# Layer 0 beside layer 1: which engine adds the blocks of exponentials into the softmax sums

## Chip, cores and metric

The kernel runs on one core of a Trainium2 chip. The metric is device time in microseconds (us), the median of three runs; before the change it is 3661.74 us (3661.73 to 3662.2). The profiled execution spans 3658.6 us. PE is TensorE, DVE is VectorE, ACT is ScalarE, POOL is GpSimd and SP is the queue that issues the DMAs.

## The reference

The input is a float32 image batch of 4 x 256 channels x 48 x 48. Four layers follow one another, each as `x = x + layer(group_norm(x))`:

- Layer 0 is attention over the 2304 pixels with 8 heads of 64 channels. Queries and keys are normalised to length one.
- Layer 1 is a pooled, blurred, depthwise attention gate.
- Layer 2 is attention with one head of 64 channels, then a batch norm over the whole batch.
- Layer 3 is a channel gate, a depthwise 3x3 convolution and an instance norm.

What matters here is layer 0:

```python
sim = jnp.einsum('bhdi,bhdj->bhij', q, k) * SCALE
attn = jax.nn.softmax(sim, axis=-1)
out = jnp.einsum('bhij,bhdj->bhid', attn, v)
out = out.transpose(0, 1, 3, 2).reshape(b, HEADS * DIM_HEAD, h, w)
return jnp.einsum('oc,bchw->bohw', w_out, out) + b_out[None, :, None, None]
```

The softmax needs, for every query, the sum of its 2304 exponentials. That sum is what the change is about.

## The kernel before

**Units.** Layer 0 is cut into units. A unit is one image (`b`, 0 to 3), one pair of heads (`p`, 0 to 3) and one chunk of 384 queries (`c`, 0 to 5), so there are 96 units, 24 for each image. A unit goes over 18 blocks of 128 keys, in 9 groups (`g`) of two blocks. For each block PE multiplies keys and queries (`scores`, L270), ACT takes the exponential of the 128 x 768 result into a tile `pt` (L276; there are eight such tiles), and PE multiplies it with the values (`weigh`, L290).

**Sums.** The same `pt` tiles are added up into one 128 x 768 tile `acc` for each unit, by `add_up` (L295 to L316). For groups in the unit's `paired` set, GpSimd first adds the group's two blocks into a tile `half` (L301), and VectorE adds `half` to `acc` one group later. For other groups, VectorE adds both blocks itself. The first add of a unit has no `acc` yet and adds two blocks (L310). With `PAIRED = (1, 3, 5, 7)` the adds fall like this:

| | GpSimd | VectorE |
|---|---|---|
| group 0 | | L310, one add of two blocks |
| groups 1, 3, 5, 7 | one pair add each (L301) | nothing |
| groups 2, 4, 6, 8 | | L316 three times: the waiting `half`, then two blocks |

That is 4 adds on GpSimd and 13 on VectorE for each unit.

**Order.** The order of the instructions on every engine is written by hand: the function `attend` (L427) walks over all groups of all units, and engines work their own list in that order. One step of it is called a slot here; a unit has slots 0 to 8. In a slot come, in this order: the scores of this group, `add_up` of the group before, what is `due`, then what fills TensorE (`fills`) and the steps of layer 1 that run beside it (`lanes`), and last the `weigh` of the group before:

```python
            for j in range(g * G, (g + 1) * G):
                scores(u, j)
            do(fills, t, lambda rank: rank < 1)
            if prev is not None:
                add_up(*prev)
            do(due, t)
```

So the adds of group g are in slot g + 1, and those of group 8 in slot 0 of the next unit.

**After a unit.** `last` (L407) sets the rest of a unit by slots counted from slot 0 of the next unit: in slot 2 GpSimd adds two halves of the output (`fold`, L367); in slot 3 TensorE sums `acc` over the partitions (`total`, L323); in slot 5 VectorE inverts the sums (`invert`, L343 to L358) and DMAs spread them over the partitions; in slot 0 of the unit after (9 slots on) GpSimd multiplies with them (`divide`, L371); and in slot 2 of that unit (11 slots on) comes `out_proj`. It has two parts, each a product on TensorE (L648, two matmuls) and an add on VectorE from PSUM into the image `X` (L653). The PSUM tiles `pj` come from a pool of two, shared with the projections of the next pair of heads. In slot 2 their order on TensorE is: a query projection (L566), the values (L597), `out_proj` part 0, a key projection (L566), `out_proj` part 1. So part 1 takes the `pj` tile of part 0, and its matmul waits until L653 of part 0 has read it.

**Layer 1 beside layer 0.** While the units of image b run, for b = 1, 2, 3, layer 1 of image b - 1 runs in the same slots. Its steps on VectorE are, for each of two channel halves: maxima and blur (L765 to L797, two steps in slot 2 and one each in slots 3, 5, 6 and 8, some 18 us in all), rounds of tap products (written by ACT, L826, summed by VectorE with one reduce of 1.48 us, L849, in slots 2, 4, 6 and 8), and the gate (L936 to L956). Image 0 has nothing of layer 1 beside it.

Of the kernel before, what the change touches and what calls it, by code (L numbers as in the profile page):

```python
# [22 lines left out]
SL = 384  # L23
# [42 lines left out]
PAIRED = (1, 3, 5, 7)  # L66
# [8 lines left out]
def usual_path(  # L75
# [566 lines left out]
    def out_proj(b, p, c, pair, o):  # L642

        cols = slice(c * SL, (c + 1) * SL)

        def part(k):
            ps = pj_tile()
            nc.tensor.matmul(  # L648
                ps[:, :SL], lhsT=wo[:, p, k * P : (k + 1) * P], rhs=o["o"], start=True,
                stop=True,  # L650
            )
            xs = X[b][:, k, cols]
            nc.vector.scalar_tensor_tensor(  # L653
                xs, ps[:, :SL], pair["bo"][:, k : k + 1], xs, ALU.add, ALU.add
            )

        return [((2.5 if b else 0, 4)[k], lambda k=k: part(k)) for k in range(NK)]

    def l0_unit(b, p, c, pair):
        hold = {}  # L660

        def o_tile():
            hold["o"] = op.tile([P, SL], F32, tag="o", name="o")
            return hold["o"]

        return {
            "pt": {}, "qc": slice(c * SL, (c + 1) * SL), "paired": PAIRED,
            "soon": b == B - 1 and p == NPAIR - 1 and c == NCH - 1,
            "scale": 1.0, "of": pair, "o": o_tile,
            "after": out_proj(b, p, c, pair, hold),  # L670
        }
# [555 lines left out]
    for i, (b, p) in enumerate(order):  # L1227
# [30 lines left out]
        if p == 1 and b + 1 < B:  # L1258
            others.append((gn(b + 1, norms0[b + 1], placed=True), NSL + 1, 0, n - 3 * NG))
        phases.append(([l0_unit(b, p, c, pairs[b][p]) for c in range(NCH)], work, others))  # L1260

    n = L2C * NG
# [1261 lines left out]
```

## Time and profile before

| | PE | DVE | ACT | POOL |
|---|---|---|---|---|
| busy us of the 3658.6 us span | 3499.3 | 2617.0 | 2381.9 | 1389.8 |
| share | 96% | 72% | 65% | 38% |

The main rows for the adds, over the whole span (layer 2 uses the same lines):

| line | engine, operation | count | mean |
|---|---|---|---|
| L301 | POOL, half = pt + pt | 477 | 1990 ns |
| L316 | DVE, acc = acc + pt | 792 | 1215 ns |
| L316 | DVE, acc = acc + half | 459 | 1035 ns |
| L310 | DVE, acc = pt + pt | 99 | 1521 ns |

A group's row in the profile gives the busy time, the mean of one instruction, and the idle time of its engine just before it with what ended most of that. A window view gives busy times for stretches of the span. The timeline gives single instructions with their start and length; a bracket holds the idle time before, and who ended it. Layer 0 beside layer 1 is the stretch from 759 us to 2945 us (72 units); from 78 us to 759 us layer 0 runs alone.

### The profile page before, as it was taken

How to read it: one execution, taken by the hardware profiler on the slowest of the kernel's cores; microseconds unless marked ns; L12 is line 12 of the kernel's file. 1: busy time of each engine (PE TensorE's matmuls, PEld its weight loads, DVE VectorE, ACT ScalarE, POOL GpSimd, SP SyncE). 2: the span in 40 equal slices, each digit the busy share in tenths (PEclk: the TensorE clock that was granted, in tenths of full speed). 3: DMA queues.
4: the chain of work that ended last, by engine and by line, in shares of the span. 5: the costliest groups of instructions: out<-in, count | busy, mean ns of one | idle time of the engine just before them, and what ended most of it. 6: DMA issues, size and time to landing. Idle time of an engine off the chain costs nothing. (4 is left out here: it accounts for less than half of the span.)

```text
span 3658.6 us, 86475 instructions
## 1 busy us (share of the span) xinstructions
PE 3499.3 (96%) x36338; PEld 1778.0 (49%) x36338; DVE 2617.0 (72%) x3227; ACT 2381.9 (65%) x3814; POOL 1389.8 (38%) x881
## 2 busy tenths in 40 slices
PE   8999999999999999999999999999999999999685
PEld 4555555454444445544444444444444445654343
DVE  3555555476989786869896868688967687576687
ACT  4665666666875886668758866687588555555353
POOL 2333333333333333333333333333333366664232
PEclk9999999999999999999999999999999999999797
DMA  2111111111111111311111111111111100000001
GB/s 91 47 25 21 27 22 25 21 25 21 26 21 25 21 26 21 77 21 25 21 25 21 25 21 26 21 26 21 30 13 30 13 6 6 6 8 4 26 39 66
DMA packets 113534, 95.52 MB, mean 26 GB/s; under 512 B 56192, under 2 KB 110064, under 8 KB 111600
## 3 DMA queue, kind: packets, MB, share of 16 engines
q1 hardware_dynamic: 110240, 87.73, 13.1%
q8 instruction: 286, 4.69, 0.5%
q10 hardware_dynamic: 2896, 2.18, 0.2%
q14 instruction: 112, 0.92, 0.1%
HBM read 56.97 MB, written 11.80 MB: 19 GB/s over the span
## 5 line engine op out<-in xcount | busy, mean ns | idle before, releaser
L276 ACT ACTIVATE pt<-sc 128x768 f32<-128x768 f32 x1944 | 1475.3, 811 | 768.2 <-PE sc L270 759.9
L301 POOL TENSOR_TENSOR half<-pt 128x768 f32<-128x768 f32 x477 | 948.7, 1990 | 1607.9 <-ACT pt L276 1512.2
L270 PE MATMUL sc<-q,k 64*64 64x384 f32 x13824 | 1273.3, 483 | 5.1 <-ACT pt L276 5.1
L290 PE MATMUL av<-pt,v 64*64 64x384 f32 x13824 | 1276.4, 484 | 0.0
L316 DVE TENSOR_TENSOR acc<-acc,pt 128x768 f32<-128x768 f32 x792 | 962.1, 1215 | 81.0 <-DVE acc L316 1.9
L270 PEld LDWEIGHTS sc<-q,k 64*64 64x64 f32 x13824 | 521.0, 133 | 607.9 <-issue 537.3
L290 PEld LDWEIGHTS av<-pt,v 64*64 64x64 f32 x13824 | 518.6, 133 | 592.2 <-issue 559.5
L316 DVE TENSOR_TENSOR acc<-acc,half 128x768 f32<-128x768 f32 x459 | 475.1, 1035 | 306.3 <-POOL half L301 305.1
L653 DVE SCALAR_TENSOR_TENSOR x<-pj,bo,x 128x384 f32<-128x384 f32 x192 | 118.3, 616 | 435.3 <-PE pj L648 434.8
L826 ACT ACTIVATE prod<-pd,wt 128x256 f32<-128x256 f32 x486 | 335.9, 761 | 0.2
L566 PE MATMUL pj<-xs,w 128*128 128x384 f32 (+1 forms) x720 | 275.4, 505 | 0.9 <-POOL xs L510 0.9
L371 POOL TENSOR_TENSOR o<-o,rinv 128x384 f32<-128x384 f32 x95 | 119.0, 1253 | 358.0 <-DMA rinv<-rinv 336.1
L566 PEld LDWEIGHTS pj<-xs,w 128*128 128x128 f32 x720 | 124.1, 189 | 128.9 <-issue 35.9
L290 PE MATMUL av<-pt,qv 64*64 64x384 f32 x1728 | 178.0, 503 | 0.0
L648 PE MATMUL pj<-o,wo 128*128 128x384 f32 x384 | 162.0, 506 | 14.8 <-DVE x L653 7.2
L270 PE MATMUL sc<-qv,kd 64*64 64x384 f32 x1728 | 172.3, 491 | 2.4 <-ACT pt L276 2.4
L849 DVE TENSOR_REDUCE prod<-prod 128x256 f32<-128x1280 f32 x114 | 168.4, 1477 | 4.1 <-ACT prod L826 4.1
L310 DVE TENSOR_TENSOR acc<-pt 128x768 f32<-128x768 f32 x99 | 150.6, 1521 | 10.7 <-ACT pt L276 10.7
L597 PEld LDWEIGHTS pj<-w,xs 128*128 128x128 f32 x1080 | 134.5, 191 | 24.1
L597 PE MATMUL pj<-w,xs 128*128 128x128 f32 x1080 | 134.9, 275 | 0.0
L367 POOL TENSOR_TENSOR o<-raw 128x384 f32<-128x384 f32 x95 | 117.6, 1238 | 0.0
L582 ACT ACTIVATE k<-pj,bias 128x384 f32<-128x384 f32 x90 | 52.3, 581 | 95.3 <-PE pj L566 94.8
(234 smaller groups left out, 2672.0 us busy)
## 6 DMA issues: line engine op xcount, KB each, us to landing
xs<-in_x_dram SPq DMA_DIRECT2D x90, 384.0 KB
rinv<-rinv SPq DMA_DIRECT2D x208, 94.5 KB
out_dram<-x SPq DMA_DIRECT2D x6, 1152.0 KB
l<-row SPq DMA_DIRECT2D x416, 1.5 KB
w<-in_wqkv_dram SPq DMA_DIRECT2D x32, 192.0 KB
x<-in_x_dram SPq DMA_DIRECT2D x4, 1152.0 KB
x<-in_x_dram SPq DMA_DIRECT2D x9, 384.0 KB
rinv<-ls SPq DMA_DIRECT2D x208, 1.5 KB
```

The lines of the kernel that those rows point to most:

```text
L270: nc.tensor.matmul(ps[c * D : (c + 1) * D, h, :SL], lhsT=u["of"]["k"][r, j0 : j0 + D], rhs=u["of"]["q"][r, u["qc"]], start=True, stop=True,)
L276: nc.scalar.activation(pt, ps[:, :, :SL], AF.Exp, scale=u["scale"])
L290: nc.tensor.matmul(u["av"][h * D : (h + 1) * D, half, :SL], lhsT=value(u, j, h)[r], rhs=pt[r, h, :], start=j == 0, stop=j == JB - 1,)
L301: nc.gpsimd.tensor_add(half, pts[0], pts[1])
L310: nc.vector.tensor_add(u["acc"], ready[0], ready[1])
L316: nc.vector.tensor_add(u["acc"], u["acc"], term)
L371: eng.tensor_mul(o, o, u["rinv"])
L566: nc.tensor.matmul(ps[:, :n], lhsT=at["w"][:, k, t, :], rhs=xs[s][:, k, :n], start=k == 0, stop=k == NK - 1,)
L597: nc.tensor.matmul(ps[:, i * P : (i + 1) * P], lhsT=xs[s][:, k, i * P : (i + 1) * P], rhs=at["w"][:, k, 2, :], start=k == 0, stop=k == NK - 1,
L648: nc.tensor.matmul(ps[:, :SL], lhsT=wo[:, p, k * P : (k + 1) * P], rhs=o["o"], start=True, stop=True,)
L826: nc.scalar.activation(bufs[n % 3][:, :, min(n, 1) + i].rearrange("p (r c) -> p r c", c=AS), pd[:, PAD + dr : PAD + dr + AS, PAD + dc : PA ...
L849: nc.vector.tensor_reduce(to, bufs[n % 3][:, :, : min(n, 1) + len(taps)], AX.X, ALU.add)
```

## The change

For the units of images 1 to 3, those that run beside layer 1, the set of paired groups is empty: VectorE adds both blocks of every group itself, and GpSimd adds no pairs there. Units of image 0 keep their pairs, and so does layer 2, which has its own setting. The aim is to take GpSimd's pair adds away from beside VectorE's work of layer 1.

```diff
         return {
-            "pt": {}, "qc": slice(c * SL, (c + 1) * SL), "paired": PAIRED,
+            "pt": {}, "qc": slice(c * SL, (c + 1) * SL), "paired": () if b else PAIRED,
             "soon": b == B - 1 and p == NPAIR - 1 and c == NCH - 1,
             "scale": 1.0, "of": pair, "o": o_tile,
```

## The prediction

> **What bounds the kernel now.** I read the page's first part, then windows by image, the waits of TensorE, the groups of VectorE by form, and a timeline. The windows below are layer 0 of image 0 alone, then images 1, 2 and 3 beside layer 1; columns are the window and its length, then the busy time and instructions of each engine.
>
> ```profile
> PE 3499.3 (96%) x36338; PEld 1778.0 (49%) x36338; DVE 2617.0 (72%) x3227; ACT 2381.9 (65%) x3814; POOL 1389.8 (38%) x881
> ...
> 77.50:759.20 681.70, 681.02 (x7400) 343.43 (x7392) 357.04 (x490) 415.07 (x659) 230.19 (x165) 1.00 0.16 28
> 759.20:1487.80 728.60, 722.20 (x7730) 355.17 (x7722) 577.62 (x672) 528.72 (x856) 267.69 (x157) 1.00 0.15 24
> 1487.80:2216.60 728.80, 721.45 (x7732) 355.47 (x7724) 572.54 (x675) 528.71 (x856) 265.15 (x158) 1.00 0.16 29
> 2216.60:2945.00 728.40, 716.69 (x7728) 351.01 (x7724) 563.66 (x653) 524.36 (x834) 261.85 (x156) 1.00 0.14 21
> ```
>
> TensorE sets the time. It idles 0.7 us in image 0 and 6.4, 7.4 and 11.7 us in images 1 to 3: 25.5 us is all the idle time that any edit there can return. VectorE is busy 79% beside layer 1, so it matters only where TensorE waits for it. TensorE's waits in the stretch 760 to 2945 us (total, times, longest):
>
> ```profile
> PE pj L648 <- DVE x L653: 6.9, 6, 1.7
> ...
> PE pj L196 <- DVE x L653: 2.8, 3, 1.0
> ...
> PE pj L1029 <- DVE bias L983: 2.5, 1, 2.5
> ...
> PE pj L566 <- POOL xs L510: 0.9, 1, 0.9
> ```
>
> VectorE's lateness costs 6.9 + 2.8 + 2.5 = 12.2 us, in ten places. Nowhere does ScalarE wait for a `pt` tile. Why VectorE is late, by its groups and GpSimd's in the same stretch:
>
> ```profile
> L316 DVE TENSOR_TENSOR acc<-acc,pt 128x768 f32<-128x768 f32 x576 | 738.8, 1283 | 58.0 <-DVE acc L316 1.4 <-ACT prod L826 0.9 <-ACT pt L276 0.5
> L316 DVE TENSOR_TENSOR acc<-acc,half 128x768 f32<-128x768 f32 x288 | 284.7, 989 | 108.8 <-POOL half L301 108.8
> ...
> L310 DVE TENSOR_TENSOR acc<-pt 128x768 f32<-128x768 f32 x72 | 120.8, 1678 | 1.0 <-ACT pt L276 1.0
> L653 DVE SCALAR_TENSOR_TENSOR x<-pj,bo,x 128x384 f32<-128x384 f32 x144 | 88.7, 616 | 276.5 <-PE pj L648 276.0
> ...
> L301 POOL TENSOR_TENSOR half<-pt 128x768 f32<-128x768 f32 x290 | 587.3, 2025 | 1058.4 <-ACT pt L276 990.6 <-DVE acc L316 27.9 <-DVE rs L808 12.0
> ```
>
> The same add of 768 elements takes 1283 or 1678 ns on average, but 0.95 or 0.96 us where the timeline shows it undisturbed. One slot 2 shows the rest, first VectorE, then GpSimd, then TensorE:
>
> ```profile
> 1154.18 0.95 DVE L316 TENSOR_TENSOR acc<-acc,half 128x768 f32<-128x768 f32 x1
> 1155.24 2.63 DVE L316 TENSOR_TENSOR acc<-acc,pt 128x768 f32<-128x768 f32 x2
> 1157.79 2.57 DVE L310 TENSOR_TENSOR acc<-pt 128x768 f32<-128x768 f32 x1
> 1160.28 2.22 DVE L765 TENSOR_TENSOR t<-x 128x1222 f32<-128x1222 f32 x1
> ...
> 1162.51 0.60 DVE L653 SCALAR_TENSOR_TENSOR x<-pj,bo,x 128x384 f32<-128x384 f32 x1
> ...
> 1155.54 1.52 POOL L371 TENSOR_TENSOR o<-o,rinv 128x384 f32<-128x384 f32 x1 [6.20 <-DMA rinv<-rinv]
> 1157.02 2.52 POOL L301 TENSOR_TENSOR half<-pt 128x768 f32<-128x768 f32 x1
> 1159.50 1.71 POOL L367 TENSOR_TENSOR o<-raw 128x384 f32<-128x384 f32 x1
> ...
> 1159.14 0.81 PE L648 MATMUL pj<-o,wo 128*128 128x384 f32 x2
> ...
> 1163.17 0.91 PE L648 MATMUL pj<-o,wo 128*128 128x384 f32 x2 [1.75 <-DVE x L653]
> ```
>
> L310 takes 2.57 us: it stands still until `half` ends at 1159.54, and then needs 0.82 us. L765 waits the same way for the fold (L367). So part 0's L653, ready at 1159.95, starts at 1162.51, and TensorE idles 1.75 us.
>
> **What the Trainium skill says.** "SBUF — State Buffer", section "SBUF: two separate sides": VectorE and GpSimd share one port pair; a VectorE instruction with two SBUF inputs and a GpSimd instruction that reads SBUF exclude each other, and whoever starts first holds it to its end. The trace agrees: L310 above ends 0.82 us after `half`. "GPSIMD Engine Reference", section "4.1 Engine selection": a two-input add is about twice slower on GpSimd. The trace agrees: single pair adds of 1.81 us against 0.95. "VectorE: DVE Perf Modes", section "Why `tensor_tensor` can't do 2×_2P or 4×": a float32 add of two tensors runs at one element per cycle, so the moved adds have no faster form; 0.95 us for 768 elements agrees.
>
> **The change part by part, for one of the 72 units.**
>
> *Removed:* four L301 on GpSimd (2.03 us each) and four adds of `half` on VectorE. *Added:* eight adds of `pt` on VectorE. Net four adds more, at 0.96 us plus the 0.10 us between dependent adds (two of them take 2.02 us from start to end): 4 x 1.06 = 4.2 us.
>
> *Returned, 1: waits for the port pair.* Against 0.96 and 0.95 us, the groups hold 576 x (1.283 - 0.96) + 72 x (1.678 - 0.95) + 288 x (0.989 - 0.95) = 186 + 52 + 11 = 249 us of standing still. Folds and divides stay (94.8 + 89.9 us of GpSimd time against 587.3 us of pair adds, so 24%); I take 76% as the pairs': 189 us, 2.6 us a unit, and some 0.3 us more on layer 1's own two-input steps. *Returned, 2: idle time for GpSimd's `half`:* 108.8 / 72 = 1.5 us a unit. Together 4.4 us returned against 4.2 us added: on average VectorE's load stays near 80%, and nothing of that alone reaches the end.
>
> *In the units where TensorE waits* more is returned. In the unit ending with the slot 2 above (from 1133.1 us, where VectorE had nothing left over), pair adds block a `pt` add by 1.42 us (3.44 us for two, not 2.02), another by 1.53 (3.55 for two), L791 by 1.65 (2.37 us, against 0.72 undisturbed) and L310 by 1.62: 6.2 us, against 4.2 us added. L653 then comes about 2.0 us sooner, enough for the 1.75 us stall. Divide and fold still block 0.6 and 0.8 us.
>
> *Moved:* VectorE's three adds in slots 3, 5, 7 and 0 become two in every slot from 2 on. Behind the two new adds in slot 2 is L653, and TensorE waits for that; their blocks are ready at about the slot's start (1155.00 us above, when the scores begin), and L653's matmul ends 4.9 us later (1159.95), so two adds of 2.1 us fit where VectorE has caught up: it idles 276 us / 144 = 1.9 us ahead of each L653. In slots 4, 6 and 8 the reduces L849 are queued behind them; these feed later taps with a whole round of slack (VectorE waited 4.1 us for taps in all). `pt` tiles of paired groups are held by VectorE's lag instead of GpSimd's; with eight tiles the slack is two to three slots.
>
> *Sum.* Of the 12.2 us I take 9 to 10 as gone, and leave 2 to 3 us: each image has one or two late units in which the pair adds blocked less than in the one worked out, so that some 0.5 us of their wait may stay. L983 (2.5 us late) stood behind adds held 4.13 instead of 2.02 us and an L310 of 1.74 us, and keeps next to nothing. POOL's L510 (0.9 us) has no pair add ahead of it. Total about 11 us: 3661.7 - 11 = 3651. Slower matmuls just after two of the long stalls (five gaps of about 0.3 us at 1165 us, four at 2773 us, together near 3 us) may add to it.
>
> **The rivals.**
>
> *A, the stalls stay (same).* For it: L653 is late because of the order in VectorE's list, and now two adds stand ahead of it. Against it: the pair adds' lock waits are larger than those adds in the late units. Time: 3661.7 less 0 to 5 us, say 3659.
>
> *B, VectorE becomes the bound (slower).* For it: in 1100 to 1200 us it is already 90.5% busy, and the maxima units (about four for an image, twelve in all) have no slack; if fold and divide take up the port waits instead, only the 1.5 us of idle time comes back, and 4.2 - 1.5 = 2.7 us a unit lands on TensorE: 12 x 2.7 = 32 us, 3694 us; half of it gives 3678. Against it: fold and divide run 1.0 us each where undisturbed, far less than the pairs.
>
> *C, more comes back.* All 25.5 us of idle time and 3 us of slow matmuls: 3633 us. Against it: the 29 waits for ScalarE (4.9 us in the same view) come from its own list, and the short gaps between projections have no wait at all.
>
> **How the numbers follow.** My forecast has 0.68, A 0.18, B 0.09, C 0.05. Faster by over 0.2% (below 3654.4 us) is C and nearly all of my forecast: 0.69; same 0.22; slower 0.09. The range reaches from 3640 (all DVE waits, slow matmuls and part of C) to 3662 (A).
>
> **What would show it.** L316 on `pt` near 1.0 to 1.05 us in images 1 to 3, sixteen a unit; L310 near 1.0 to 1.3 us; no L301 between 790 and 2935 us; VectorE's busy time within 5% of 1714 us in that stretch; TensorE's waits for L653 below 4 us; each image 3 to 5 us shorter. Wrong if L653 is late in more than ten units, if ScalarE starts to wait for `pt` tiles, or if L316 stays above 1.15 us because fold and divide take the pairs' place.

## The result, and the profile after

The changed kernel takes 3645.32 us (median of four runs, 3643.28 to 3647.99), the kernel before 3661.73 us beside it. The medians differ by 16.4 us; the ratio of the runs is put at 0.9958, with a 95% interval of 0.994 to 0.9975, so the gain is between 9 and 22 us. Forecast were 3651 us, in a range from 3640 to 3662.

The windows of images 1, 2 and 3, to be read beside those of before (window and length, then busy time and instructions of PE, PEld, DVE, ACT, POOL, then the granted clock):

```profile
757.80:1481.70 723.90, 720.00 (x7730) 355.73 (x7722) 582.40 (x768) 527.61 (x856) 73.77 (x61) 1.00 0.15 24
1481.70:2208.10 726.40, 720.86 (x7729) 355.86 (x7724) 582.09 (x770) 527.55 (x855) 73.05 (x62) 1.00 0.16 29
2208.10:2931.60 723.50, 716.10 (x7728) 351.61 (x7724) 576.35 (x748) 523.06 (x834) 76.56 (x59) 1.00 0.14 21
```

The three images took 728.6, 728.8 and 728.4 us; now they take 723.9, 726.4 and 723.5 us, so 12.0 us less. TensorE's idle time there fell from 25.5 to 16.8 us, which is 8.7 us. Its busy time fell by 3.4 us, with as many matmuls on record. The rest of the 13.9 us between the two profiles is 1.4 us ahead of image 0's first unit, where nothing was changed, and 0.5 us after these three images; single runs differ by as much. VectorE's busy time hardly moved: 1740.8 us in place of 1713.8, although it does four adds more in each of 72 units. Here is why (VectorE's groups from 760 to 2945 us, then GpSimd's from 790 to 2925 us):

```profile
L316 DVE TENSOR_TENSOR acc<-acc,pt 128x768 f32<-128x768 f32 x1152 | 1143.0, 992 | 150.4 <-ACT pt L276 73.0 <-DVE acc L316 1.9 <-ACT row L332 0.5
L310 DVE TENSOR_TENSOR acc<-pt 128x768 f32<-128x768 f32 x71 | 95.5, 1345 | 16.5 <-ACT pt L276 16.5
L653 DVE SCALAR_TENSOR_TENSOR x<-pj,bo,x 128x384 f32<-128x384 f32 x148 | 91.4, 618 | 226.2 <-PE pj L648 225.9
...
L367 POOL TENSOR_TENSOR o<-raw 128x384 f32<-128x384 f32 x70 | 97.7, 1396 | 41.6 <-ACT raw L363 40.8
L371 POOL TENSOR_TENSOR o<-o,rinv 128x384 f32<-128x384 f32 x70 | 92.9, 1327 | 1650.6 <-DMA rinv<-rinv 1650.6
```

An add of `pt` takes 992 ns in place of 1283, and 0.96 us undisturbed. VectorE now waits for ScalarE's exponentials at times (73.0 us), which means that it has caught up with them; it had waited 108.8 us for GpSimd's `half`. Of GpSimd's larger work only fold and divide are left.

How GpSimd holds up VectorE can be read off the single adds. The record of the kernel before has 572 adds of `pt` in these images. 280 of them overlap no pair add, fold or divide, and each took 0.96 us; so did each of 139 that had started before GpSimd did. Another 150 started while one of GpSimd's was running: 147 of these ended 0.81 or 0.82 us after its end. In the changed kernel 71 of the 1152 adds started so, all of them beside folds and divides.

TensorE's waits in the three images (757 to 2932 us):

```profile
PE sc L270 <- ACT pt L276: 6.0, 29, 0.2
...
PE pj L648 <- DVE x L653: 2.8, 4, 1.4
```

The rows for L196 behind L653 (2.8 us), for L1029 behind L983 (2.5 us) and for L566 behind GpSimd's L510 (0.9 us) are gone, and that for L648 behind L653 fell from 6.9 to 2.8 us. The slot 2 that the prediction worked out looks like this now (VectorE, GpSimd, TensorE):

```profile
1150.27 2.62 DVE L316 TENSOR_TENSOR acc<-acc,pt 128x768 f32<-128x768 f32 x2
1152.82 0.95 DVE L310 TENSOR_TENSOR acc<-pt 128x768 f32<-128x768 f32 x1
1153.87 2.02 DVE L316 TENSOR_TENSOR acc<-acc,pt 128x768 f32<-128x768 f32 x2
1155.81 1.43 DVE L765 TENSOR_TENSOR t<-x 128x1222 f32<-128x1222 f32 x1
...
1157.24 0.61 DVE L653 SCALAR_TENSOR_TENSOR x<-pj,bo,x 128x384 f32<-128x384 f32 x1
...
1150.56 1.52 POOL L367 TENSOR_TENSOR o<-raw 128x384 f32<-128x384 f32 x1 [0.88 <-ACT raw L363]
...
1156.09 0.81 PE L648 MATMUL pj<-o,wo 128*128 128x384 f32 x2
1156.82 1.56 PE L566 MATMUL pj<-xs,w 128*128 128x384 f32 x4
1158.22 0.81 PE L648 MATMUL pj<-o,wo 128*128 128x384 f32 x2
```

L310 takes 0.95 us (2.57 before) and L765 1.43 (2.22 before). The two new adds stand ahead of L765 and take 2.02 us. L653 starts 0.34 us after its matmul's end at 1156.90, where it started 2.56 us after it, and TensorE goes from L566 to L648 with no wait, where it idled 1.75 us.

Half of the 3.4 us of busy time comes from the clock that TensorE was granted. After the 1.75 us of idle time the kernel before ran at half speed (0.50) for 3.4 us:

```profile
1164.20:1167.60 3.40, 3.40 (x22) 1.54 (x26) 3.29 (x6) 0.00 (x0) 0.00 (x0) 0.50 0.00 0
1167.60:1180.00 12.40, 12.40 (x160) 5.52 (x156) 11.98 (x15) 7.56 (x12) 5.50 (x2) 1.00 0.07 5
```

Its record has one more such stretch in these three images, at 2771.8 us, behind the wait for L983. Two stretches of 3.4 us at half speed lose 2 x 1.7 = 3.4 us. The changed kernel has neither of them, but one of its own near the end of image 3, which loses 1.7 us:

```profile
2905.56:2908.97 3.41, 3.41 (x18) 1.10 (x21) 2.49 (x6) 0.00 (x0) 0.00 (x0) 0.50 0.00 0
```

Some later runs have a stretch at this place and some do not, with the pairs and without them. So the clock gives 1.7 us net. The other 1.7 us is spread thinly over matmuls behind waits (two of L648 take 0.91 us behind the wait of 1.75 us, and 0.81 us where there was none); it was not taken apart.

### The profile page after: what moved, and what is told of

Read it like the earlier page. It is cut to its first block, busy times and chain, and to the rows that moved or that the text cites. A ratio compares the mean times of both kernels' runs of the same rounds, so it can differ in the third digit from the quotient of the medians.

```text
span 3644.7 us, 86565 instructions
## 1 busy us (share of the span) xinstructions
PE 3493.5 (96%) x36338; PEld 1775.7 (49%) x36338; DVE 2643.3 (73%) x3515; ACT 2377.8 (65%) x3814; POOL 820.0 (22%) x593
## 3 DMA queue, kind: packets, MB, share of 16 engines
q1 hardware_dynamic: 110240, 87.73, 13.1%
## 5 line engine op out<-in xcount | busy, mean ns | idle before, releaser
L316 DVE TENSOR_TENSOR acc<-acc,pt 128x768 f32<-128x768 f32 x1368 | 1365.4, 998 | 173.4 <-ACT pt L276 73.0
L301 POOL TENSOR_TENSOR half<-pt 128x768 f32<-128x768 f32 x189 | 366.3, 1941 | 548.1 <-ACT pt L276 508.7
L653 DVE SCALAR_TENSOR_TENSOR x<-pj,bo,x 128x384 f32<-128x384 f32 x192 | 118.6, 618 | 381.0 <-PE pj L648 380.7
L316 DVE TENSOR_TENSOR acc<-acc,half 128x768 f32<-128x768 f32 x171 | 188.9, 1105 | 195.3 <-POOL half L301 194.1
L566 PE MATMUL pj<-xs,w 128*128 128x384 f32 (+1 forms) x720 | 275.4, 505 | 0.0
L566 PEld LDWEIGHTS pj<-xs,w 128*128 128x128 f32 x720 | 124.1, 189 | 127.9 <-issue 38.3
L648 PE MATMUL pj<-o,wo 128*128 128x384 f32 x384 | 160.8, 502 | 11.2 <-issue 3.6
L310 DVE TENSOR_TENSOR acc<-pt 128x768 f32<-128x768 f32 x99 | 127.4, 1287 | 25.9 <-ACT pt L276 25.9
```

What stands on the lines that cost most here:

```text
L301: nc.gpsimd.tensor_add(half, pts[0], pts[1])
L310: nc.vector.tensor_add(u["acc"], ready[0], ready[1])
L316: nc.vector.tensor_add(u["acc"], u["acc"], term)
L566: nc.tensor.matmul(ps[:, :n], lhsT=at["w"][:, k, t, :], rhs=xs[s][:, k, :n], start=k == 0, stop=k == NK - 1,)
L648: nc.tensor.matmul(ps[:, :SL], lhsT=wo[:, p, k * P : (k + 1) * P], rhs=o["o"], start=True, stop=True,)
```

## The experiments

**Theory and rivals.** PORT: GpSimd's pair adds held the port pair that VectorE's adds need; without them VectorE comes to L653 in time. ORDER: the even spread, two adds in every slot, is what helps. HALF: VectorE's standing still for `half` was the cost. Line numbers in the experiments are up to five higher than in the kernel before.

### GpSimd still makes the pairs, for nobody

```diff
         else:
+            if g in u.get("ghost", ()):
+                half = hpool.tile([P, 2, SL], F32, tag="half", name="half")
+                nc.gpsimd.tensor_add(half, pts[0], pts[1])
             ready, u["terms"] = terms + pts, []
```

> The changed kernel, but in images 1 to 3 GpSimd still makes the four pair adds of each unit, into tiles that nobody reads; VectorE keeps its new list with all 17 adds. Theory PORT (the gain comes from the port pair that the pair adds held): the waits come back, with four more adds than in the kernel before, so the time is above the kernel before: 3665 to 3700 us, the add of pt back near 1.25 us. Rival ORDER (the gain comes from two adds in every slot in place of three in every second one) and rival HALF (it comes from VectorE's no longer waiting for GpSimd's half): 3645 to 3652 us, since both stay as in the changed kernel.

3831.32 us, a ratio of 1.0463 (1.0449 to 1.0477). ORDER and HALF fall: VectorE's list is that of the changed kernel and it waits for no `half`, yet the time is 186 us more. PORT has the direction, but its 3665 to 3700 us were far too low. The window of image 1, TensorE's largest wait and its one wait for GpSimd, and the add:

```profile
758.80:1547.90 789.10, 743.55 (x7730) 355.95 (x7722) 703.76 (x765) 528.72 (x855) 277.36 (x157) 0.97 0.13 22
...
PE pj L651 <- DVE x L656: 94.0, 43, 5.2
...
PE pj L569 <- POOL xs L513: 0.5, 1, 0.5
...
L319 DVE TENSOR_TENSOR acc<-acc,pt 128x768 f32<-128x768 f32 x1060 | 1323.3, 1248 | 103.1 <-ACT pt L276 29.0 <-DVE acc L319 1.4 <-ACT row L335 0.5
```

The add is back at 1248 ns, and VectorE's busy time for an image is 703.8 us in place of 582.4. That is 89% of 789 us. The image is 65.2 us longer. TensorE's idle time grew from 3.9 to 45.6 us, which is 41.7 us of that; its busy time grew by the other 23.6 us, of which 22 us are the clock (13 windows of 3.41 us at half speed). Up to 2990 us TensorE waits some 120 us for VectorE and 0.5 us for GpSimd, so it is not that folds or divides come late behind the pair adds.

### The same list with bursts

```diff
+        elif g in u.get("late", ()):
+            ready, u["terms"] = terms, pts
         else:
             ready, u["terms"] = terms + pts, []
```

> The changed kernel, but VectorE adds the two blocks of groups 1, 3, 5 and 7 one group later, so that its adds stand where they stood before: four in slots 3, 5, 7 and 0, none in slots 2, 4, 6 and 8. GpSimd makes no pairs. PORT: as the changed kernel, 3640 to 3650 us, with no more waits for L653 than there. ORDER: the gain is lost, 3657 to 3665 us. HALF: as the changed kernel.

3644.72 us, 0.9957 (0.9944 to 0.9971): the same as the changed kernel, with 0.9 us of waits for L653. ORDER falls a second time. The waits for L653 fell from 2.8 to 0.9 us with no adds in slot 2, but the time did not change.

### GpSimd busy with work that reads nothing

```diff
+                for _ in range(3):
+                    nc.gpsimd.memset(half, 0.0)
```

> As the run with unread pair adds, but in their places GpSimd does three memsets of the same 128 x 768 tile (about 0.74 us each, worked out from the memset of 128 x 784 of 0.75 us), which read nothing from SBUF. PORT, as the Trainium skill has it (only a GpSimd instruction that reads SBUF excludes a VectorE instruction with two SBUF inputs): as the changed kernel, 3643 to 3650 us, add of pt at 0.97 to 1.02 us. If a busy GpSimd of any kind slows VectorE: 3655 to 3700 us and adds of 1.1 us or more.

3644.86 us, 0.9956 (0.9942 to 0.9969).

```profile
L320 DVE TENSOR_TENSOR acc<-acc,pt 128x768 f32<-128x768 f32 x1154 | 1156.6, 1002 | 152.0 <-ACT pt L276 75.0 <-DVE acc L320 1.9 <-ACT pd L813 0.5
...
L308 POOL MEMSET half<- 128x768 f32 x864 | 630.9, 739 | 33.2
```

GpSimd is as busy as with the pairs (630.9 us, where the pair adds took 587.3), and VectorE's add stays at 1002 ns. So it isn't a busy GpSimd as such that costs. That it has to be one that reads SBUF is what the Trainium skill states ("SBUF — State Buffer", "SBUF: two separate sides"), and this run agrees; a GpSimd instruction with a single SBUF input was not run beside these adds.

### Which units pay

```diff
-            "paired": () if b else PAIRED,
+            "paired": () if b and p * NCH + c in LOADED else PAIRED,
```

with `LOADED = (0, 1, 2, 3, 6, 10, 11, 12, 13, 14, 20, 21)`.

> Pairs are dropped only in the 12 units of each of the images 1 to 3 that have maxima, gate or statistics of layer 1 beside them; the other 12 (rounds of tap products or nothing) keep them. Theory LATE UNITS (only the few units where TensorE waited for VectorE matter): all of the gain, 3643 to 3650 us. Rival EVERY UNIT (each unpaired unit gives its share): about half of it, 3651 to 3656 us.

3651.72 us, 0.9975 (0.9965 to 0.9984): by its time the rival EVERY UNIT. TensorE's waits speak against it:

```profile
PE pj L649 <- DVE x L654: 3.8, 7, 1.0
...
PE pj L1030 <- DVE bias L984: 2.2, 1, 2.2
...
PE pj L567 <- POOL xs L511: 1.0, 1, 1.0
```

The long stalls at units 13 of images 1 to 3, and those of 0.9 to 1.0 us at unit 3, lie in unpaired units and are gone. Those left stand in or just behind units that kept their pairs: at unit 6 of images 1 and 2, behind unit 5 (1.0 us each), the wait for L510 at unit 18 of image 2, and the wait for L983 at unit 18 of image 3 with its half-speed matmuls (6.8 us of them, so 3.4 us lost). By this reading a few late places make the gain, and the list, chosen by what of layer 1 runs beside each unit, missed the units at four of them. A run with the list mended was not made.

### What four adds cost where the port is free

VectorE makes four unread pair adds a unit itself, on top of its 17:

```diff
+                nc.vector.tensor_add(half, pts[0], pts[1])
```

> The changed kernel, but VectorE also makes the four pair adds of each unit in images 1 to 3, into tiles that nobody reads (0.95 us each, so 3.8 us a unit, 91 us an image); GpSimd makes none. It asks why the run with unread pairs on GpSimd went to 3831 us. Theory LOAD (VectorE's list was too long: its busy time per image rose from 582 us in the changed kernel to 704 us): 91 us on top of 582 us is 673 us, nearly as much, so 3700 to 3810 us with TensorE's waits for L653. Rival GPSIMD LATE (folds and divides came late behind the pairs): 3644 to 3660 us, since GpSimd is free here.

3699.29 us, 1.01 (1.0083 to 1.0117).

```profile
759.10:1499.50 740.40, 726.72 (x7730) 355.73 (x7722) 655.00 (x862) 528.43 (x855) 73.08 (x61) 0.99 0.14 24
...
PE pj L651 <- DVE x L656: 25.5, 18, 2.8
```

GPSIMD LATE falls. LOAD has the direction and the waits for L653; the time is just below its 3700 to 3810 us. VectorE is at 655 of 740 us, so 88.5%. What remains is time in which VectorE must stand still in its order: 124.1 us ahead of L653 for TensorE and 63.2 us for exponentials in the three images, and the 0.1 us between dependent adds. The run with unread pairs took another 132 us; VectorE is 153 us busier there in the three images, and 89 to 91% busy. So VectorE binds when it is 88 to 91% busy, in the six images of these two runs. By that, at 80% as in the changed kernel, there would be room for some 66 us an image (an estimate: 0.89 x 726 - 580); the 91 us of this run were too much, and the 121 us of the unread pairs far too much.

The fourth corner, 13 adds and no pairs: VectorE leaves out the second block of groups 1, 3, 5 and 7 in images 1 to 3, so the sums lack these blocks.

```diff
+            if g in u.get("skip", ()):
+                pts = pts[:1]
             ready, u["terms"] = terms + pts, []
```

> The changed kernel, but in images 1 to 3 VectorE leaves out the second block of groups 1, 3, 5 and 7, so that it has 13 adds a unit as before and GpSimd has no pairs; the sums lack these four blocks. It is the fourth corner beside the kernel before (13 adds, pairs), the changed kernel (17, none) and the run with unread pairs (17, pairs). PORT, with VectorE's list as the price: TensorE's waits for VectorE almost gone, 3638 to 3645 us, so that the four adds cost 0 to 7 us with the port pair free against some 170 us with the pair adds beside them. If the four adds cost the same in both, the time would be near 3475 us, which the work of TensorE rules out; if the pairs cost nothing at 13 adds: 3655 us or more.

3645.14 us, 0.9948 (0.9934 to 0.9961), at the upper end of what PORT gave, with 0.9 us of waits for L653:

```profile
PE pj L650 <- DVE x L655: 0.9, 2, 0.6
```

The four corners, in us (the pairs are read beside 13 adds and unread beside 17; the kernel before took 3660.2 to 3664.4 us beside these runs):

| | GpSimd makes pairs | no pairs |
|---|---|---|
| VectorE makes 13 adds | 3661.7 | 3645.1 |
| VectorE makes 17 adds | 3831.3 | 3645.3 |

The four adds cost nothing that these runs can tell without the pairs, and 170 us with them. The pairs cost 17 us beside 13 adds, and 186 us beside 17.

### VectorE doesn't wait for half

The kernel before, with every `half` added one group later:

```diff
+        elif u.get("lag"):
+            ready, u["terms"] = u.get("held", []) + pts, []
+            u["held"] = terms
+            if g == NG - 1:
+                ready, u["held"] = ready + terms, []
         else:
             ready, u["terms"] = terms + pts, []
```

> The kernel before, with its pairs on GpSimd, but in images 1 to 3 VectorE adds each half one group later than before (two after its blocks), so that it need not stand and wait for GpSimd; only group 7's half is added where it was. It takes away most of the 108.8 us for which VectorE waited for half beside layer 1, and leaves the pair adds and their hold on the port pair. PORT: little, since the units where TensorE waits had no wait for half: 3656 to 3663 us, the add of pt still 1.25 us or more. HALF: the gain, 3645 to 3652 us.

3664.77 us, 1.0006 (0.9997 to 1.0014): no gain, so HALF falls. The record of the kernel before says the same: in the 30 us ahead of each of nine of the ten late places VectorE never waited for `half`. The tenth, of 0.59 us at 2920 us, is still there after the change.

```profile
PE pj L653 <- DVE x L658: 7.8, 9, 1.6
...
L321 DVE TENSOR_TENSOR acc<-acc,pt 128x768 f32<-128x768 f32 x578 | 610.7, 1057 | 156.4 <-ACT pt L276 112.5 <-DVE acc L321 0.9 <-ACT prod L831 0.5
L321 DVE TENSOR_TENSOR acc<-acc,half 128x768 f32<-128x768 f32 x288 | 337.5, 1172 | 10.7
...
L315 DVE TENSOR_TENSOR acc<-pt 128x768 f32<-128x768 f32 x72 | 104.8, 1455 | 0.5 <-ACT pt L276 0.5
```

All of VectorE's 108.8 us of waiting for `half` is gone (no such releaser is left up to 2945 us); it waits for ScalarE instead, and TensorE waits as before. One expectation missed: the add of `pt` came down to 1057 ns, with the adds of `half` up to 1172. Against 0.96 and 0.95 us the three groups still stand 56 + 64 + 36 = 156 us, where it was 249 us. So over a third of the port waits went too, at no gain. Sums over all units don't tell the time; what stands ahead of L653 in late units does.

### Other places

> The changed kernel, but image 0, with nothing of layer 1 beside it, has no pairs either. TensorE idled 0.7 us in its 681.7 us and VectorE was busy 52%, so there is nothing to return and room for the four adds: the same as the changed kernel, 3642 to 3649 us, image 0 at 681 to 683 us. If port waits cost something where TensorE doesn't wait: image 0 shorter by 2 us or more.

`"paired": ()` for every unit: 3645.55 us, 0.9953 (0.9936 to 0.9969), image 0 at 681.8 us where it had 681.7. In this image, where TensorE doesn't wait for VectorE, pairs are neither good nor bad.

Layer 2 with `"paired": PAIRED if b == B - 1 else ()`:

> The changed kernel, and in layer 2 the units of images 0 to 2 (nine pair adds each on GpSimd, with the last part of layer 1 beside them) have no pairs either. In the changed kernel VectorE waits 54.6 us for half there and its adds of half take 1353 ns in place of 0.95 us. If the same account carries over (time in that stretch, 451 us, is set by VectorE and GpSimd getting in each other's way): 5 to 20 us less, 3625 to 3640 us. If VectorE's nine more adds a unit (about 9 us, 81 us in all) outweigh that, as they would where nothing hides them: 3650 to 3700 us.

3630.68 us, 0.9912 (0.9895 to 0.9928). Layer 2, from the last `weigh` of layer 0 to its own last one, goes from 450.8 to 437.1 us. With `"paired": PAIRED` in layer 2:

> As the run without pairs in layer 2, but with pairs in groups 1, 3, 5 and 7 (four on GpSimd, 13 adds on VectorE), as layer 0 had before. Between the changed kernel and the run without pairs if the account is one of load shared between two engines; below both if an even split suits that stretch: 3630 to 3645 us.

3647.99 us, 0.9959 (0.9945 to 0.9973), layer 2 at 451.1 us: an even split gives nothing, and the time is above the forecast. Then `"paired": ()` for all of layer 2:

> The changed kernel with no pairs in layer 2 either, its last image included (which the run without pairs in images 0 to 2 of layer 2, 3630.7 us, left at four pairs). In that image TensorE waits at the ends of units only; the same or a little less: 3625 to 3633 us. If VectorE's four more adds stand before the sums at the ends of its three units: up to 3640 us.

3627.53 us, 0.9905 (0.989 to 0.9921), the lowest of all, 34 us less than the kernel before; layer 2 takes 434.1 us. Its interval overlaps that of the run with pairs in layer 2's last image. VectorE makes nine adds a unit more in layer 2's images 0 to 2, as the columns of these windows over most of layer 2 show (the changed kernel, then this one):

```profile
2931.00:3370.00 439.00, 405.73 (x4559) 233.58 (x4552) 308.31 (x358) 233.56 (x375) 262.40 (x145) 0.97 0.06 6
```

```profile
2931.00:3360.00 429.00, 409.98 (x4638) 238.68 (x4640) 313.70 (x456) 235.70 (x378) 70.86 (x54) 0.97 0.06 6
```

VectorE has 98 instructions more and 5.4 us more of busy time, and GpSimd 192 us less. This looks like layer 0 again, but it was not shown: here the waits for `half` (54.6 us) went as well, and the two were not taken apart.

With bursts in layer 0 on top:

> As the run before it, with VectorE's adds in layer 0 of images 1 to 3 in bursts of four, as in the run on bursts, where TensorE's waits for L653 were 0.9 us and not 3.1 us: 2 to 3 us less than the run before it, so 3623 to 3631 us; no difference if those waits are made up elsewhere.

3629.36 us, 0.9909 (0.9894 to 0.9924): no better. The waits that bursts save can't be seen between runs.

## Why the prediction was right, step by step

- **The bound.** Right: VectorE's lateness at L653, L196 and L983 and GpSimd's at L510 cost TensorE 13.1 us, and 10.3 us of that went. The 29 waits for ScalarE stayed (4.9 us, now 6.0), as was held against rival C. TensorE's idle time as a whole fell by 8.7 us, since these and other small waits grew.
- **The port waits.** Right: of 249 us of standing still on the adds, 189 us were to go. Against the same 0.96 and 0.95 us, 37 + 28 = 65 us are left, so 184 us went. The add of `pt` fell to 992 ns (1000 to 1050 forecast). L310 at 1345 ns missed its 1000 to 1300: 34 of the 36 slow ones stand beside a fold, which no longer queues behind a pair on GpSimd and so comes sooner.
- **Four adds for 4.2 us, 4.4 us returned.** Right in its balance: VectorE was busy for 78% of these images (79% in the prediction) and is now for 80%, 27 us more in 72 units. Not all terms were right: by the sum of durations the adds rose by 95 us and VectorE's other steps fell by 60 us, 0.8 us a unit where 0.3 was forecast.
- **The idle time for `half`, counted as returned.** This was worth nothing by itself, as the run with a later `half` shows. It was right to put the gain into the late units.
- **The unit worked out.** L653 was to come 2.0 us sooner; its delay behind its matmul fell from 2.56 to 0.34 us, by 2.2 us.
- **Two adds ahead of L653 in slot 2.** The risk was real but small: 2.8 us of waits are left, against the 2 to 3 forecast. They fall to 0.9 us with bursts and with 13 adds, both of which put fewer adds into slot 2. The largest, 1.4 us, has two gate steps of layer 1 there as well, and is in image 2, which gained 2.4 us where 3 to 5 were forecast.
- **The sum.** Forecast 11 us, measured 16.4 (9 to 22), and 13.9 between the profiles, of which the three images have 12.0. That it comes so close is in part luck. The term left at "may add", the matmuls' half speed after long waits, was sized right for the two stretches that went (3.4 us) and belonged in the sum, but a new stretch took 1.7 us back. The rest of the difference is no larger than that between single runs.
- **Rival B.** The forecast of 3678 to 3694 us for a VectorE that stays blocked was too mild: with the pairs still there, the change would have cost 170 us. VectorE binds at 88 to 91% busy, not at 100%, and long stalls halve the clock on top.
- **No faster form for the moved adds.** Right: they took 0.96 us each where nothing held them up. That a float32 add of two tensors runs at the slowest of the rates stands in the Trainium skill's page "VectorE: DVE Perf Modes" under "Mode 2×_2P — use both read ports for one tensor"; the section that the prediction names tells why two of the faster modes are out.

## What to carry to other kernels

Work moved to a second engine is not free for the first when the two get in each other's way at SBUF, as VectorE and GpSimd did here: count how much longer the first one's own instructions become (here 0.3 us on each add), and move the work back where that exceeds what it saves. Judge it in the slot where the bounding engine waits, not by the sum over all units; over a third of the port waits could go at no gain. And look for the load at which an engine with a fixed order binds (here 88 to 91% busy): four adds that were free below it cost 170 us above it, ten times what the change gained.

## What the runs showed of the hardware

- TensorE's granted clock fell to 0.50 for 3.4 us after idle times well under that length: after 1.75 us in the kernel before, and after 26 of 27 idle times over 2.2 us in layer 0 of the run with unread pairs. "TensorE: Matmul & The Clock Gate" in the Trainium skill (section "Part 1: The HAM clock gate (the "warmup" mystery)") tells of an idle window of some 3.4 us; here shorter idle times did it, and the measurement decides.
- What counts is how the idle time falls on a raster. In all fourteen traces the clock changes only on a raster of 3.41 us, fixed within a trace. Take the windows of 3.41 us between its marks that ran at full speed, in layer 0 beside layer 1. All 30 with more than 2 us of idle time were followed by a window at half speed, and none with less than 1.19 us was; in between both happened. The wait of 1.74 us that ended at 2619 us in the kernel before lay across two windows, and the clock stayed full. So whether a stall near 2 us costs 2 us or 3.7 us depends on where it falls.
- A VectorE add of two SBUF tiles that started while GpSimd was adding or multiplying two tiles ended 0.81 or 0.82 us after GpSimd's instruction (147 of 150). One that started first, or met none, took 0.96 us (419 of 419).
- GpSimd's memsets (739 ns for 128 x 768) leave VectorE's two-input adds at 1002 ns on average; its two-input adds bring them to 1248 ns.
